# Four places in a four-layer kernel where instructions are put in another order

## Chip, cores and metric

The kernel runs on one core of a Trainium2 chip, as one program. The metric is device time in microseconds (us), lower is better. Instructions are issued in order on each engine: PE (TensorE, the matrix unit), DVE (VectorE), ACT (ScalarE), POOL (GpSimd) and SP (SyncE, which only starts DMA transfers). PE can run at a reduced clock; the profile shows the clock that was granted, 1.00 being full speed.

## The reference

A float32 residual stream `x` of 1024 tokens by 512 features goes through four layers, each added to `x` behind a layer norm without weights:

1. Linear attention with a memory: queries of 8 heads are `elu(q)+1`, multiplied by a memory matrix and divided by a normaliser, then projected.
2. A mixture of 8 low-rank experts (rank 16) beside a dense product. A router takes the two best experts of each token; the dense product has a bias.
3. A Mamba2 layer. An input projection gives gate, x, B, C and dt. x, B and C go through a causal convolution of four taps and silu. In each chunk of 128 tokens y = (C.B times decay) x plus what the chunk before passes on; then y times silu(gate), an RMS norm over 8192 features, and an output projection.
4. A mixture of 4 low-rank experts (rank 8), one per token.

```
def _layernorm(x, axis=-1, eps=1e-05):
    m = jnp.mean(x, axis=axis, keepdims=True)
    v = jnp.var(x, axis=axis, keepdims=True)
    return (x - m) / jnp.sqrt(v + eps)
```

The weight of C.B between tokens s ≤ l of a chunk is exp(cs[l] - cs[s]), with cs the running sum of dt·A. The kernel makes it as exp(-relu(cs[s] - cs[l])); the relu is what is called "clipping" here.

## The kernel before, in words

`x` lies in 8 tiles of 128 tokens by 512 features. Most of the work keeps tokens along the free dimension: `xnT` holds the normalised activations transposed (features on partitions, 1024 tokens free), and PE multiplies against it in 512-token halves.

The code is written for a framework that places the waits: it runs the instructions of an engine in the order in which the program, with a scheduler, puts them, and each waits for the instructions that make its inputs or that still use its buffer. `tc.issue_after(ins)` is a hand-written order: instructions under it are queued behind `ins` on their own engine. Buffers come from pools with a fixed number of copies, so a new tile waits until its buffer's last reader is done.

**First norm (L105 to L125, L308).** For each tile DVE takes statistics (`bn_stats` L108, `bn_aggr` L110), ACT the square root (L112), DVE the reciprocal (L114). The normalised tile `xn` is made on DVE for tiles 0, 3 and 6 (L121) and on ACT for the others (L118 makes its offset on DVE, L119 is the ACT operation). PE transposes four blocks (`ln_ps`, L124) and ACT copies them into `xnT` (L125). L308 calls this tile by tile, and the order on DVE comes out as statistics of several tiles ahead of the rest of the first. Then `zr` is spread (L313) and the queries of 8 heads follow (`ps_q`, L97), whose first half needs `xnT` of tiles 0 to 3. The weights of the output projection are summed on POOL (L295 to L297).

**Attention's projection and second norm (L375 to L397).** PE makes `ps_o` for each tile (L377), DVE adds it to `x` (L392), and the norm of the tile before follows. The norm of tile 7 comes after the loop (L395), then the bias of layer 2 is added to each tile on POOL (L397).

**Router (L148 to L198).** `lora_mixture` runs over the tiles: `f_psl` (L158) gives router scores and low-rank products of a tile, which DVE copies (L165, L166). A callback `ready(t)` can be called ahead of each tile; the first mixture has none. Then `f_pso` (L175), `route_top2` on DVE, transposes (L191) and the expert products (L194).

**Mamba2 (L435 on).** 72 units follow each other: 8 groups, each with one unit for B and C and 8 pairs of heads. `stage_a` of unit n projects (L609), keeps parts of products on ACT (L620), convolves on DVE (L648, L652) and takes silu on ACT (L660, L714, L715). `load_sums` loads 1.5 MB of running sums into `cst` (L726, on SP). `stage_t` of a B/C unit makes C.B on PE (`ps_g`, L740, L747), and from it the tile `gt`: masked on DVE (L757, L763), and copied on ACT (L769). `stage_t` of a pair transposes x (`ps_xt`, L775) and scales it (`xdt` L778, `xdr` L785), then calls `decays` (L797): parts 0 and 1 are 8 clippings each on ACT (L808); part 2 is two exponentials (L814) and two products with `gt` on DVE (L816). `stage_c` multiplies (`ps_y`, L831, L839), adds D·x on DVE (L847) and squares on ACT (L849); `stage_d` multiplies by the gate (L857) and adds the squares to `ssq` (L858). A table `early` (L1005) sets the stages of units 0 to 6; from there on `turn` runs stage_c of n-2 and stage_t of n-1 between the projections of unit n, and `put_off` marks the pairs whose clippings are placed apart.

**Output products and tail.** The output projection of two pairs at a time is seven products `ps_p` (L916), taken in the order 0, 1, 2, 4, 5, 6, 3 and once for each half m. `add_up` (L921) copies each on ACT to a `prod` buffer (L925; three of them) and POOL starts the DMA that adds it to DRAM (L926). In the last unit, `add_up` empties the list `taken` of the last four products behind the last exponential (L1060). After the loop come, in this order, the remaining silu (L1079), the last pair's 16 clippings, `load_prods` (L1086, SP: seven sums loaded as `out10` to `out13`, `out00` to `out03`) and the last two pairs' stages. `put_together` (L944) forms the sums: m=1 on POOL, m=0 on DVE, behind `last["cst"]`. PE meanwhile runs `ps_out` (L1128) of the last four pairs; then come the RMS norm's sums (L1156), `finish` (L1163) of each tile and the last mixture.

```
        with issue_after(last["silu"]):
            for part in range(2):
                decays(N - 1, part)
        with issue_after(last["sums"]):
            load_prods(1)
            load_prods(0)
```

Of the kernel before, what the change touches and what calls it, by code (L numbers as in the profile page):

```python
# [33 lines left out]
P = 128  # L34
# [19 lines left out]
def model_kernel(ctx: ExitStack, tc: tile.TileContext, a: dict, out: bass.AP):  # L54
# [48 lines left out]
                )  # L103

    def layernorm(t, psum, xnp, on_act=False):  # L105

        st = small.tile([P, 6], F32, tag="ln_st", name=f"ln_st{t}")
        nc.vector.bn_stats(st, x[t])  # L108
        mv = small.tile([P, 2], F32, tag="ln_mv", name=f"ln_mv{t}")
        nc.vector.bn_aggr(mv, st)  # L110
        sd = small.tile([P, 1], F32, tag="ln_sd", name=f"ln_sd{t}")
        nc.scalar.activation(sd, mv[:, 1:2], AF.Sqrt, bias=eps, scale=1.0)  # L112
        rs = small.tile([P, 1], F32, tag="ln_rs", name=f"ln_rs{t}")
        nc.vector.reciprocal(rs, sd)  # L114
        xn = xnp.tile([P, DM], F32, tag="xn", name=f"xn{t}")
        if on_act:
            sh = small.tile([P, 1], F32, tag="ln_sh", name=f"ln_sh{t}")
            nc.vector.tensor_scalar(sh, mv[:, 0:1], rs, -1.0, ALU.mult, ALU.mult)  # L118
            nc.scalar.activation(xn, x[t], AF.Identity, bias=sh, scale=rs)  # L119
        else:  # L120
            nc.vector.tensor_scalar(xn, x[t], mv[:, 0:1], rs, ALU.subtract, ALU.mult)  # L121
        ps = psum.tile([P, 512], F32, tag="mm1", name=f"ln_ps{t}")
        for k in range(KT):
            nc.tensor.transpose(ps[:, toks(k)], xn[:, toks(k)], ident)  # L124
        marks["xnT"] = nc.scalar.copy(xnT[:, :, toks(t)], ps.rearrange("p (k t) -> p k t", k=KT))  # L125
# [128 lines left out]
    with ExitStack() as c0:  # L254
# [50 lines left out]
        nc.gpsimd.dma_start(out=f0_up, in_=a["f0_up"])  # L305
        nc.gpsimd.dma_start(out=f0_bias, in_=a["f0_bias"].to_broadcast([P, DM]))

        for t in range(NT):  # L308
            layernorm(t, Both, xns, on_act=t % 3 != 0)


        zr = cw.tile([P, NKV, 32], F32, tag="zr", name="zr")
        nc.vector.tensor_copy(zr, bcast(z, [P, NKV, 32]))  # L313
        sig = [cw.tile([P, NTOK], F32, tag=f"sig{h}", name=f"sig{h}") for h in range(NKV)]

        def queries(h):
# [69 lines left out]
        for t in range(NT):  # L386
# [5 lines left out]
            nc.vector.tensor_tensor(x[t], outs.pop(t), x[t], ALU.add)  # L392
            if t >= 1:
                layernorm(t - 1, Both, act)
        layernorm(NT - 1, Both, act)  # L395
        for t in range(NT):
            nc.gpsimd.tensor_tensor(x[t], x[t], f0_bias, ALU.add)  # L397

        def route_top2(lg):
            E = 8  # L400
# [27 lines left out]
            if t >= 1:  # L428
                layernorm(t - 1, Both, act)

        lora_mixture("f0", 8, 16, f0_base, f0_cat, f0_up, route_top2, Both, act, then_norm)
        layernorm(NT - 1, Both, act)


    with ExitStack() as c1:  # L435
# [9 lines left out]

        last = {"pe": None, "one": None, "two": None, "adt": None, "bar": None, "keep": None, "cst": None, "silu": None, "exp": None, "sums": None}

        def issue_after(ins):  # L450
            return tc.issue_after(ins.ins) if ins else nullcontext()
# [247 lines left out]
        def stage_a(n):  # L699
            kind, i = units[n]  # L700
            raw = b2.tile([P, NTOK], F32, tag="raw", name=f"raw{n}")
            first = xyp.tile([P, NTOK], F32, tag="xy", name=f"xT{n}")
            second = b3.tile([P, NTOK], F32, tag="sg", name=f"sg{n}")
            if kind == "bc":
                raw2 = xyp.tile([P, NTOK], F32, tag="xy", name=f"raw2_{n}")
                pa = yield from project(n, raw, raw2)
                nc.scalar.copy(raw2[:, :512], pa)
                later(n, lambda: conv_silu(raw, 64 + i, first))
                later(n, lambda: conv_silu(raw2, 72 + i, second))
                held[n] = [first, second]  # L710
            else:
                pa = yield from project(n, raw, second)
                later(n, lambda: conv_silu(raw, i, first))
                nc.scalar.activation(second[:, :512], pa, AF.Silu)  # L714
                last["silu"] = nc.scalar.activation(second[:, 512:], second[:, 512:], AF.Silu)  # L715
                held[n] = {"xT": first, "sg": second}
            prefetch(n + 2)
            yield

        def load_sums(n):  # L720

            kind, j = units[n]
            if kind == "bc":
                return
            cst = b2.tile([P, 2, NT + NB, P], F32, tag="cst", name=f"cst{j}")
            last["sums"] = nc.sync.dma_start(  # L726
                out=cst.rearrange("p h c l -> p h (c l)"),
                in_=cs_d[2 * j : 2 * j + 2, :].unsqueeze(0).to_broadcast([P, 2, (NT + NB) * P]),
            )
            held[n].update(cst=cst)  # L730

        def stage_t(n):
            kind, i = units[n]
            if kind == "bc":
                bt, ct = held.pop(n)

                ps = Psum.tile([P, 2, 512], F32, "mm2", f"ps_g0{i}")
                p1 = Psum.tile([P, 512], F32, "mm1", f"ps_g1{i}")
                for b in range(NB):
                    last["pe"] = nc.tensor.matmul(  # L740
                        flat(ps)[:, b * SEQ : (b + 1) * SEQ],
                        lhsT=bt[:, toks(2 * b)],
                        rhs=ct[:, b * SEQ : (b + 1) * SEQ],
                        start=True,
                        stop=True,
                    )
# [16 lines left out]
                nc.vector.tensor_tensor(  # L763
                    gv[:, :, 1, :],
                    p1.rearrange("p (b l) -> p b l", l=P),
                    bcast_mid(tri_le, [P, NB, P]),
                    ALU.mult,
                )
                nc.scalar.copy(gt[:, NT:, :], chunks(flat(ps))[:, :, 1, :])  # L769
                group[i] = gt  # L770
                return
            j, hd = i, held[n]
# [16 lines left out]
                ALU.mult,  # L789
            )  # L790
            hd["xdt"], hd["xdr"] = xdt, xdr
            for part in range(2 if n in put_off else 3):
                decays(n, part)

        decayed, put_off = set(), set()

        def decays(n, part):  # L797


            if not 0 <= n < len(units) or units[n][0] == "bc" or (n, part) in decayed:  # L800
                return
            decayed.add((n, part))
            j, gr = units[n][1], group[units[n][1] // PPG]
            m = held[n]["cst"]
            if part < 2:
                h = 2 * j + part
                for c in range(NT):
                    nc.scalar.activation(  # L808
                        m[:, part, c, :], m[:, part, c, :], AF.Relu, bias=cs[:, c, h : h + 1], scale=1.0
                    )  # L810
                return
            mf = m.rearrange("p h c l -> p h (c l)")
            for hh in range(2):
                last["exp"] = nc.scalar.activation(mf[:, hh], mf[:, hh], AF.Exp, scale=-1.0)  # L814
            for hh in range(2):
                last["cst"] = nc.vector.tensor_tensor(  # L816
                    mf[:, hh], mf[:, hh], gr.rearrange("p c l -> p (c l)"), ALU.mult
                )
# [99 lines left out]

        taken = []

        def add_up():  # L921

            for ps, m, p, over in taken:
                st = osp.tile([P, 512], F32, tag="prod", name=f"prod{over[-1]}_{m}_{p}")
                nc.scalar.copy(st, ps)  # L925
                nc.gpsimd.dma_start(  # L926
                    out=prod_d[m][p // 2][p % 2], in_=st, accum_op=ALU.add if over[0] else ALU.bypass
                )
            taken.clear()

        prods = {}

# [95 lines left out]
        for n in range(len(units)):  # L1028
# [28 lines left out]
            turn(n, 1)  # L1057
            next(a_steps)
            out_products(share - share // 2)
            with issue_after(last["exp"] if n == len(units) - 1 else None):  # L1060
                add_up()
            if share and not todo:
                end_out(began - 1)
            turn(n, 2)
# [3 lines left out]
                    decays(n - 1, 2)  # L1068
            if n == max(early):
                last["bar"] = None  # L1070
            if 1 < n < len(units):
                load_sums(n)


# [2 lines left out]
        N = len(units)  # L1077
        with issue_after(last["silu"]):
            for step in behind_keeps:  # L1079
                last["silu"] = step()  # L1080
        behind_keeps.clear()
        with issue_after(last["silu"]):
            for part in range(2):
                decays(N - 1, part)
        with issue_after(last["sums"]):
            load_prods(1)  # L1086
            load_prods(0)
# [160 lines left out]
```

## Time and profile before

| | us |
|---|---|
| median of 3 runs | 1812.0 (1811.17 to 1812.17) |
| the profiled execution's own time | 1810.48 |
| its span, first to last instruction | 1808.8 |
| PE busy | 1768.5 (98%) |
| DVE busy | 1305.8 (72%) |
| ACT busy | 1187.4 (66%) |
| POOL busy | 721.2 (40%) |

The mean granted clock of PE is 0.996. The span holds 21019 instructions, and the DMA engines move 245.45 MB.

How to read it: times in profile lines are us from the span's start unless marked ns. A timeline line gives start, duration, engine, line of the kernel, operation, output<-inputs, shapes, and how many instructions in a row it sums up (x); in brackets stands how long the engine was idle before and what ended that (`<-DVE xn L121`: it waited for the instruction of line 121 on DVE). The chain of waits is followed back from the last instruction: at each step, to what released it. SPq, DVEq and so on are the engines' sequencers. Matmul ends are modelled, and the rows of one engine overlap slightly for that reason.

### The profile page before, as it was taken

Reading aid. Unit: us, or ns where it says so; the run is one execution under the profiler, and the core shown is the slowest. Engines: PE = TensorE matmul, PEld = TensorE weight load, DVE = VectorE, ACT = ScalarE, POOL = GpSimd, SP = SyncE. Lnnn points to the kernel's source line nnn. Section 1 sums busy time; section 2 is a strip of 40 time slices with the busy share of each in tenths; the row PEclk is TensorE's granted clock in tenths of the full one; section 3 lists DMA queues with packets and bytes.
Section 4 is the critical chain, followed back from the end, with each engine's and each line's share of the span. In section 5 each row is a group of like instructions: output and inputs, shape, how many; then the busy total and the mean of one; then the engine's idle time right before and its main releaser. Section 6 shows DMA issues by size and latency. Waiting matters only on the chain.

```text
span 1808.8 us, 21019 instructions
## 1 busy us (share of the span) xinstructions
PE 1768.5 (98%) x7520; PEld 918.0 (51%) x7520; DVE 1305.8 (72%) x1423; ACT 1187.4 (66%) x2135; POOL 721.2 (40%) x689
## 2 busy tenths in 40 slices
PE   7999988999999999999999999999999999999989
PEld 4445544555555555555555455555555555555554
DVE  4744898886877777777877687868786877777662
ACT  4311369766877588847875777668766877588740
POOL 5410342353444444443444434534444444444220
PEclk9999999999999999999999999999999999999999
DMA  8310134355566545555555446554554566546831
GB/s 314 130 37 24 56 121 152 134 145 117 154 159 150 125 123 147 147 149 145 151 148 146 111 135 157 150 134 135 146 145 112 148 166 149 125 128 152 193 121 47
DMA packets 82810, 245.45 MB, mean 136 GB/s; under 512 B 9921, under 2 KB 10945, under 8 KB 73361
## 3 DMA queue, kind: packets, MB, share of 16 engines
q1 hardware_dynamic: 50240, 175.91, 27.9%
q0 software_dynamic: 31888, 67.14, 21.9%
q8 instruction: 60, 0.98, 0.2%
q10 hardware_dynamic: 576, 1.05, 0.2%
q14 instruction: 46, 0.37, 0.1%
HBM read 182.17 MB, written 61.90 MB: 135 GB/s over the span
## 4 chain that ended last, share of the span: by engine, by line
PE 88%; DVE 5%; ACT 3%; DMA 2%; issue 2%; POOL 1%; SPq 0%; DVEq 0%; ACTq 0%; POOLq 0%
PE pa L609 25%; PE ps_p L916 19%; PE pd L609 12%; PE pb L609 6%; PE ps_y L831 6%; PE ps_o L377 3%; PE ps_q L97 3%; PE ps_xt L775 3%; PE ps_y L839 3%; PE f_pso L175 2%; DVE xT L652 1%; PE f_pso L212 1%; ACT cst L808 1%; PE ps_out L1128 1%; DMA cst<-cs_d 1%
## 5 line engine op out<-in xcount | busy, mean ns | idle before, releaser
L926 POOL DMA_DIRECT2D prod_d<-prod x217 | 189.8, 907 | 583.1 <-ACT prod L925 550.3
L808 ACT ACTIVATE cst<-cst,cs 128x128 f32<-128x128 f32 x1024 | 313.0, 398 | 5.7 <-DMA cst<-cs_d 5.7
L652 DVE SCALAR_TENSOR_TENSOR xT<-raw,convw,xT 128x1020 f32<-128x1020 f32 (+2 forms) x216 | 278.6, 1291 | 4.1
L816 DVE TENSOR_TENSOR cst<-cst,gt 128x1536 f32<-128x1536 f32 x128 | 222.2, 1766 | 13.1 <-ACT cst L814 13.1
L594 POOL TENSOR_TENSOR wsum<-win 128x256 f32<-128x256 f32 x72 | 116.4, 1616 | 264.1 <-DMA win<-in_win 218.6
L849 ACT ACTIVATE xdt<-xT 128x1024 f32<-128x1024 f32 x64 | 67.7, 1058 | 194.1 <-DVE xT L847 194.1
L814 ACT ACTIVATE cst<-cst 128x1536 f32<-128x1536 f32 x128 | 189.4, 1484 | 1.0
L632 DVE TENSOR_TENSOR raw<-pb,keep 128x512 f32<-128x512 f32 x72 | 49.7, 690 | 161.9 <-PE pb L609 158.8
L831 PE MATMUL ps_y<-cst,xdt 128*64 128x128 f32 x2048 | 160.6, 277 | 6.0 <-issue 3.7
L916 PE MATMUL ps_p<-xT,wout 128*128 128x512 f32 x360 | 165.0, 593 | 0.0
L636 DVE TENSOR_TENSOR raw<-pd,keep 128x512 f32<-128x512 f32 x72 | 49.7, 690 | 152.9 <-PE pd L609 125.6
L620 ACT COPY keep<-pa 128x512 f32<-128x512 f32 x144 | 84.8, 589 | 102.6 <-PE pa L609 102.6
L609 PE MATMUL pa<-xnT,wsum 128*128 128x512 f32 x288 | 145.0, 627 | 4.2 <-ACT keep L620 4.2
L831 PEld LDWEIGHTS ps_y<-cst,xdt 128*64 128x64 f32 x2048 | 119.3, 138 | 55.6 <-issue 52.3
L925 ACT COPY prod<-ps_p 128x512 f32<-128x512 f32 x217 | 122.3, 580 | 36.9 <-PE ps_p L916 17.9
L609 PE MATMUL pa<-tok,win 128*128 128x512 f32 x288 | 135.7, 593 | 1.9 <-DVE sg L639 1.9
L609 PE MATMUL pd<-tok,wsum 128*128 128x512 f32 x288 | 136.6, 592 | 0.0
L609 PE MATMUL pa<-xnT,win 128*128 128x512 f32 x288 | 135.8, 592 | 0.6 <-DVE raw L632 0.6
L609 PE MATMUL pa<-tok,wsum 128*128 128x512 f32 x288 | 135.5, 593 | 0.7 <-POOL wsum L597 0.5
L609 PE MATMUL pd<-xnT,wsum 128*128 128x512 f32 x288 | 135.5, 592 | 0.0
L609 PE MATMUL pb<-xnT,win 128*128 128x512 f32 x288 | 135.3, 592 | 0.0
L880 POOL TENSOR_TENSOR osum<-wout,wout 128x256 f32<-128x256 f32 x30 | 106.5, 3553 | 21.4 <-DMA wout<-in_wout 20.9
(228 smaller groups left out, 3111.9 us busy)
## 6 DMA issues: line engine op xcount, KB each, us to landing
cst<-cs_d SPq DMA_DIRECT2D x64, 1536.0 KB, 6.8
prod_d<-prod POOLq DMA_DIRECT2D x217, 256.0 KB, 4.9
win<-in_win SPq DMA_DIRECT2D x144, 256.0 KB, 3.2
wout<-in_wout SPq DMA_DIRECT2D x64, 256.0 KB, 4.1
wo_s<-in_wo POOLq DMA_DIRECT2D x8, 1024.0 KB, 6.0
rb<-rd_d SPq DMA_DIRECT2D x8, 512.0 KB, 4.1
out<-prod_d SPq DMA_DIRECT2D x6, 512.0 KB, 8.7
wq<-in_wq SPq DMA_DIRECT2D x8, 256.0 KB, 4.6
```

The lines of the kernel that those rows point to most:

```text
L594: op(v[:, 0], w[:, 1, 0:2], w[:, 1, 2:4], ALU.add)
L609: last["pe"] = nc.tensor.matmul(ps, lhsT=wt[:, k, :], rhs=tk[:, k, :], start=start and k == 0, stop=k == 1, skip_group_check=not start,)
L620: last["keep"] = nc.scalar.copy(c, ps)
L652: nc.vector.scalar_tensor_tensor(d[:, :, k:], src[:, :, : SEQ - k], convw[:, i, TAPS - 1 - k : TAPS - k], d[:, :, k:], ALU.mult, ALU.add,)
L808: nc.scalar.activation(m[:, part, c, :], m[:, part, c, :], AF.Relu, bias=cs[:, c, h : h + 1], scale=1.0)
L814: last["exp"] = nc.scalar.activation(mf[:, hh], mf[:, hh], AF.Exp, scale=-1.0)
L816: last["cst"] = nc.vector.tensor_tensor(mf[:, hh], mf[:, hh], gr.rearrange("p c l -> p (c l)"), ALU.mult)
L831: last["pe"] = nc.tensor.matmul(flat(py)[e, toks(c)], lhsT=xdt[:, c, e], rhs=m[:, hh, c, :], start=True, stop=c % 2 == 0,)
L880: op(v[:, 0], e[:, 256:], o[:, 256:], ALU.add)
L916: last["pe"] = nc.tensor.matmul(ps, lhsT=w, rhs=y, start=i == over[0], stop=i == over[-1])
L925: nc.scalar.copy(st, ps)
L926: nc.gpsimd.dma_start(out=prod_d[m][p // 2][p % 2], in_=st, accum_op=ALU.add if over[0] else ALU.bypass)
```

## The change

- `layernorm` becomes a generator `norm_steps` in two steps (statistics with square root; the rest). The first norm runs step 1 of tile t, then step 2 of tile t-1, each queued behind the DVE instruction before (`marks["ln"]`); `zr` is queued behind the last. Other callers of `layernorm` run both steps at once.
- The second norm of tile 7 and its bias add move into a callback of the router, called ahead of its tile 3.
- For unit 1, the clippings and what follows are queued behind the copy of `gt` on ACT.
- In the last unit, `load_sums` is called earlier in the program, `add_up` takes three of the four products, then the 16 clippings follow, queued behind the third copy, then the fourth product is copied, queued behind the last clipping. The clippings after the loop are gone.

```
     def layernorm(t, psum, xnp, on_act=False):
+        for _ in norm_steps(t, psum, xnp, on_act):
+            pass
+
+    def norm_steps(t, psum, xnp, on_act=False):
...
-        nc.vector.bn_aggr(mv, st)
+        marks["ln"] = nc.vector.bn_aggr(mv, st)
...
         nc.scalar.activation(sd, mv[:, 1:2], AF.Sqrt, bias=eps, scale=1.0)
+        yield
...
-        for t in range(NT):
-            layernorm(t, Both, xns, on_act=t % 3 != 0)
+        norms = deque()
+        for t in range(NT + 1):
+            if t < NT:
+                norms.append(norm_steps(t, Both, xns, on_act=t % 3 != 0))
+                with tc.issue_after(marks["ln"].ins) if t else nullcontext():
+                    next(norms[-1])
+            if t:
+                with tc.issue_after(marks["ln"].ins):
+                    next(norms.popleft(), None)
...
-        nc.vector.tensor_copy(zr, bcast(z, [P, NKV, 32]))
+        with tc.issue_after(marks["ln"].ins):
+            nc.vector.tensor_copy(zr, bcast(z, [P, NKV, 32]))
...
-        layernorm(NT - 1, Both, act)
-        for t in range(NT):
+        def add_bias(t):
             nc.gpsimd.tensor_tensor(x[t], x[t], f0_bias, ALU.add)
+
+        for t in range(NT - 1):
+            add_bias(t)
+
+        def last_norm(t):
+            if t == 3:
+                layernorm(NT - 1, Both, act)
+                add_bias(NT - 1)
...
-        lora_mixture("f0", 8, 16, f0_base, f0_cat, f0_up, route_top2, Both, act, then_norm)
+        lora_mixture("f0", 8, 16, f0_base, f0_cat, f0_up, route_top2, Both, act, then_norm, last_norm)
...
-                nc.scalar.copy(gt[:, NT:, :], chunks(flat(ps))[:, :, 1, :])
+                last["gt"] = nc.scalar.copy(gt[:, NT:, :], chunks(flat(ps))[:, :, 1, :])
...
-            for part in range(2 if n in put_off else 3):
-                decays(n, part)
+            with issue_after(last["gt"] if n == 1 else None):
+                for part in range(2 if n in put_off else 3):
+                    decays(n, part)
...
-        def add_up():
-
-            for ps, m, p, over in taken:
+        def add_up(most=7):
+
+            for ps, m, p, over in taken[:most]:
...
-                nc.scalar.copy(st, ps)
+                last["prod"] = nc.scalar.copy(st, ps)
...
-            taken.clear()
+            del taken[:most]
...
-            with issue_after(last["exp"] if n == len(units) - 1 else None):
-                add_up()
+            if n == len(units) - 1:
+                load_sums(n)
+                with issue_after(last["exp"]):
+                    add_up(3)
+                with issue_after(last["prod"]):
+                    for part in range(2):
+                        decays(n, part)
+                with issue_after(last["relu"]):
+                    add_up()
+            add_up()
...
-            if 1 < n < len(units):
+            if 1 < n < len(units) - 1:
                 load_sums(n)
...
             for step in behind_keeps:
-                last["silu"] = step()
+                step()
         behind_keeps.clear()
-        with issue_after(last["silu"]):
-            for part in range(2):
-                decays(N - 1, part)
```

`last["relu"]` is the last clipping, and a pair's tiles are now put into `held` piece by piece, since `load_sums` of the last unit comes before its projections are named.

As built, the engines' queues differ from those of the kernel before in this way. DVE: statistics and rest of the first norm alternate; the router's copies of tiles 0 and 1 stand within the norm of tile 7; in the tail the first product with `gt` stands ahead of L857. PE: one `ln_ps` group fewer ahead of the first queries; `f_psl` of tiles 0 to 2 ahead of the last `ln_ps`. ACT: the `gt` copy ahead of unit 1's clippings; the last clippings ahead of the last `prod` copy; one table load less. POOL: three sums of `put_together` ahead of the last store. SP: `out01` is started after `out02`, `out03` and the first `f1_base`.

More of the change, by code (lines that the diff above doesn't have):

```diff
@@ L117, in layernorm @@
             sh = small.tile([P, 1], F32, tag="ln_sh", name=f"ln_sh{t}")
-            nc.vector.tensor_scalar(sh, mv[:, 0:1], rs, -1.0, ALU.mult, ALU.mult)
+            marks["ln"] = nc.vector.tensor_scalar(sh, mv[:, 0:1], rs, -1.0, ALU.mult, ALU.mult)
             nc.scalar.activation(xn, x[t], AF.Identity, bias=sh, scale=rs)
         else:
-            nc.vector.tensor_scalar(xn, x[t], mv[:, 0:1], rs, ALU.subtract, ALU.mult)
+            marks["ln"] = nc.vector.tensor_scalar(xn, x[t], mv[:, 0:1], rs, ALU.subtract, ALU.mult)
         ps = psum.tile([P, 512], F32, tag="mm1", name=f"ln_ps{t}")
@@ L444, in tile @@
                 return {"mm2": psum2, "mm1": psum1, "in": psumi}[tag].tile(shape, dt, tag=tag, name=name)
-        last = {"pe": None, "one": None, "two": None, "adt": None, "bar": None, "keep": None, "cst": None, "silu": None, "exp": None, "sums": None}
+        last = {"pe": None, "one": None, "two": None, "adt": None, "bar": None, "keep": None, "cst": None, "silu": None, "exp": None, "sums": None, "gt": None, "prod": None, "relu": None}
         def issue_after(ins):
@@ L715, in stage_a @@
                 last["silu"] = nc.scalar.activation(second[:, 512:], second[:, 512:], AF.Silu)
-                held[n] = {"xT": first, "sg": second}
+                held.setdefault(n, {}).update(xT=first, sg=second)
             prefetch(n + 2)
@@ L729, in load_sums @@
             )
-            held[n].update(cst=cst)
+            held.setdefault(n, {})["cst"] = cst
         def stage_t(n):
@@ L807, in decays @@
                 for c in range(NT):
-                    nc.scalar.activation(
+                    last["relu"] = nc.scalar.activation(
                         m[:, part, c, :], m[:, part, c, :], AF.Relu, bias=cs[:, c, h : h + 1], scale=1.0
```

## Prediction

> **What bounds the kernel now.** The page first. It gives TensorE (PE) 1768.5 us busy in a span of 1808.8, and its chain of waits says which engine the end was waiting for:
>
> ```profile
> PE 88%; DVE 5%; ACT 3%; DMA 2%; issue 2%; POOL 1%; SPq 0%; DVEq 0%; ACTq 0%; POOLq 0%
> ```
>
> PE issues the same matmuls in both kernels (only their order moves), so an edit is worth what it takes off PE's gaps and late start (1808.8 - 1768.5 = 40 us in all) and off its half-speed stretches. I therefore read the timeline of PE, then those of ACT, DVE and POOL, at the four places of the change. From 14 to 140 us and from about 330 to 1710 us PE hardly stops, so time won ahead of such a stretch stays won.
>
> The chain of waits, the first norm:
>
> ```profile
> 11.90 0.56 ACT xnT L125
> 12.46 0.71 ACT xn L119
> 13.18 0.97 ACT xnT L125 x2
> 14.19 2.84 PE ps_q L97 x6
> ```
>
> The first query waits for the copies of tiles 2 and 3, and ACT makes an xn between them. Timeline of PE, the router:
>
> ```profile
> 139.48 0.60 PE L124 MATMUL ln_ps<-ident,xn 128*128 128x128 f32 x4
> 142.55 0.66 PE L124 MATMUL ln_ps<-ident,xn 128*128 128x128 f32 x4 [2.47 <-DVE xn L121]
> 143.04 7.58 PE L158 MATMUL f_psl<-f_cat,xnT 128*128 128x136 f32 x64
> ```
>
> PE stands 2.47 us for the last norm with the router of seven ready tiles behind it. Timeline of ACT, then of PE, at the first C.B:
>
> ```profile
> 253.99 0.69 ACT L808 ACTIVATE cst<-cst,cs 128x128 f32<-128x128 f32 x2 [3.15 <-DMA cst<-cs_d]
> 254.59 1.04 ACT L660 ACTIVATE xT<-xT 128x1024 f32<-128x1024 f32 x1
> 255.53 0.39 ACT L808 ACTIVATE cst<-cst,cs 128x128 f32<-128x128 f32 x1
> 255.83 0.56 ACT L769 COPY gt<-ps_g 128x512 f32<-128x512 f32 x1
> ```
>
> ```profile
> 256.44 1.97 PE L775 MATMUL ps_xt<-ident,xT 128*128 128x128 f32 x8 [4.18 <-ACT gt L769]
> ...
> 278.40 3.68 PE L609 MATMUL pa<-xnT,wsum 128*128 128x512 f32 x4 [2.77 <-ACT keep L620]
> ```
>
> ACT waits 3.15 us for a load, and the gt copy that PE needs is queued behind that wait. The tail, timelines of ACT, POOL, DVE and PE:
>
> ```profile
> 1715.08 0.58 ACT L925 COPY prod<-ps_p 128x512 f32<-128x512 f32 x1 [4.43 <-DMA prod_d<-prod]
> ...
> 1716.99 4.77 ACT L808 ACTIVATE cst<-cst,cs 128x128 f32<-128x128 f32 x16
> ```
>
> ```profile
> 1721.89 1.28 POOL L950 TENSOR_TENSOR out<-out,out 128x512 f32<-128x512 f32 x1 [0.18 <-DMA out<-prod_d]
> 1723.24 2.15 POOL L951 TENSOR_TENSOR out<-out,out 128x512 f32<-128x512 f32 x1
> ```
>
> ```profile
> 1722.74 1.50 DVE L857 SCALAR_TENSOR_TENSOR xT<-xT,normw,sg 128x1024 f32<-128x1024 f32 x1 [5.86 <-ACT xdt L849]
> 1724.17 2.30 DVE L858 TENSOR_TENSOR ssq<-ssq,xdt 128x1024 f32<-128x1024 f32 x1
> ...
> 1728.12 5.05 DVE L816 TENSOR_TENSOR cst<-cst,gt 128x1536 f32<-128x1536 f32 x2
> ```
>
> ```profile
> 1733.23 0.90 PE L831 MATMUL ps_y<-cst,xdt 128*64 128x128 f32 x5 [2.29 <-DVE cst L816]
> ```
>
> ACT waits 4.43 us for a store, the 16 clippings stand behind it, and PE ends up waiting for DVE's two products of them.
>
> **Part 1, first norm: 0.4 us gained (-1.3 to +1.0).** No instruction is added. DVE now finishes tile t-1 before the statistics of t+1. I walked the three queues with the rows' durations (statistics 0.66, aggregate 0.17, 1/sd 0.14, sd 0.29, xn 0.53 on DVE and 0.81 on ACT, copy 0.56, 0.04 between dependents) and the landings of x (4.6 to 8.9). The first transpose comes near 6.9 instead of 8.82. But ACT's queue still ends sd5, xn4, xnT2, xnT3: from 11.2 on, 0.2 + 0.8 + 0.5 + 0.6 is 13.2, against 14.15 measured (14.06 in the same walk of the old order). One transpose group fewer stands before the first query, one more inside the queries; by the time the fourth 512-token half starts, the walk has 18.05 against 18.42: 0.4. Upper end, the 1.0 of the first query. Lower end: the transposes now come in pieces from 6.9 on, and the clock may still be halved at 13.2. The shortest half-speed stretch in the clock's record is 3.41 us (278.48 to 281.90); one of that length loses half of it, 1.7, less the 0.4 gained: -1.3. The zr copy moved behind the norm is read by L336, tens of us later; POOL's L296 sums end near 62, before L368 needs them at 73.
>
> **Part 2, last norm within the router: 2.3 (1.9 to 2.5).** The same instructions; the 64 router passes take 7.42 (143.04 to 150.46), 0.93 a tile. Tiles 0 to 2 now run 139.92 to 142.70. The chain of tile 7 is add 0.70, statistics 0.70, aggregate 0.20, sd 0.30, 1/sd 0.17, xn 0.56; two pairs of DVE copies (0.45 in all) now lie in it, so xn7 is ready at about 142.97, the transposes start at 143.0 (0.49 to the next row, as before), and five tiles (4.64) end at 148.13 instead of 150.46. What is late next is the DVE chain of the route: it ends at 157.32, 3.4 before L191 at 160.76, and both shift together, so L175 still covers it. The bias add of tile 7 keeps its place as POOL's last. If the clock dropped in the gap it would show in the row at 143.04, and it did not.
>
> **Part 3, C.B copy ahead: 1.7 (0.8 to 3.3).** On ACT the order becomes silu, silu, gt, 16 clippings. L757 ends at 253.91; gt runs 253.95 to 254.51, ps_xt starts at 254.55 (1.89 earlier). Queued behind gt are the clippings: their load lands at 253.99, so they lose 0.4 of start, but the second silu now sits in the wait; their two exps end at 263.4 instead of 264.4. Next late is ACT itself: keep L620, which ended the 2.77 gap, comes at 277.1, 1.3 earlier. ps_y ends 1.9 earlier or, if the half-speed stretch that followed the gap goes too, up to 3.3. Between ACT's 1.3 and PE's 1.9 lies 1.7 with the earlier load of the next cst; the lower end is ACT's 0.95 with nothing else, rounded down. Windows of PE's clock (columns: stretch, PE, PEld, DVE, ACT, POOL busy, clock, DMA share, GB/s):
>
> ```profile
> 276.00:278.00 2.00, 0.00 (x0) 0.00 (x0) 2.00 (x2) 2.00 (x3) 0.00 (x0) 1.00 0.76 240
> 279.00:280.00 1.00, 1.00 (x2) 0.34 (x1) 1.00 (x1) 0.30 (x1) 0.00 (x0) 0.50 0.90 381
> ```
>
> After a gap of 2.77 us PE ran at 0.50; after 2.47 (at 142.55) it did not. [...]
>
> **Part 4, clippings ahead of the last copy: 0.3 (-1.5 to +4.6).** ACT: the load of cst63 lands at 1712.45, so the clippings run 1712.5 to 1717.2, 4.5 earlier. The copy of product 3 follows at 1717.15 (2.1 later); the second ps_out bank is freed by it at 1717.7, 0.5 after PE wants it, and xT's silu is done at 1719.2. Both waits are covered, since DVE takes ps_xt only at 1726. The exps end at 1722.0 and 1724.3 (3.5 and 2.6 earlier), one table load saved. DVE: the first product with gt now stands ahead of L857 and waits for the first exp, with L857, L858, xdt and xdr queued behind. Its work from 1722 to the second product is 2 x 1.76 (the mean of L816 on the page) + 1.28 + 1.22 + 1.21 + 0.68 = 7.9 alone: end 1729.9. But here L816 took 2.32 and 2.83 and L858 2.30, while POOL's L951 took 2.15 and its L954 2.78 against 1.27 for its L949; the ends of one engine's operations meet the other's starts. DVE and POOL take turns, so with POOL's 10.4 us of work in the same place DVE ends at 1731 to 1733.8 against 1733.17 now. I take 1732.9, near the late end, since the second L816 (2.83) lay beside L954 (2.78) and POOL's queue isn't earlier: 0.3. The lower end is 0.6 (1733.8) and 0.9 for the store's issue, now between POOL's sums; the upper is 3.3 (1733.2 less 1729.9) and half of ps_y's half-speed stretch (1733.23 to 1735.97), 1.3.
>
> [...]
>
> The store of product 3 goes past three POOL sums: it leaves at about 1723.2 instead of 1715.95, and lands after 6.8 (this one's time before) at 1730; SP's out01 load behind it (4.06) lands at 1734, now issued behind out03 and f1_base1. DVE's L951 needs it at 1735.2. It is hidden, by 1 us.
>
> **Sum.** 0.4 + 2.3 + 1.7 + 0.3 = 4.7. The profiled execution took 1810.48 (span 1808.8): 1805.8. The median of 1812.0 lies 1.5 above it, so 1807.3. A measurement of this kernel can tell about 0.2%, 3.6 us, from no change.
>
> **Rivals.**
> - The tail carries: DVE's products slip in ahead of POOL's sums, the second ends at 1729.9, PE's gap shrinks below 2.47 and ps_y keeps its clock. 4.6 in place of 0.3: 9.0 in all, 1803.0. For: POOL's sums start only as loads land (1720.4, 1721.9). Against: the rows of alternation. 0.15.
> - The gains shrink: the queries start at half clock (-1.3) and ACT holds part 3 at 0.8 to 1.0. 2.3 + 0.9 + 0.3 - 1.3 = 2.2, about 1809.8, within 0.2%. For: ACT's idle stretch after the clippings is small. Against: in the trace the transposes fell from 0.213 to 0.107 us at about 12.2, 3.4 after the first; now the first is 6.3 ahead of the query. 0.21.
> - Slower: the late store. With 10.1 us to land (as the store of product 6 took, 1709.00 to 1719.10) it lands at 1733.3; an out01 load of 12.5 (as out10, 1703.99 to 1716.48) ends at 1745.8, 10.6 behind L951. The last pair's L847, L857 and L858 are queued behind it on DVE, and PE's L1156 waits for those: the other parts' 4.4 less 10.6 is 6 lost, about 1818. It decides from L951 past 1743.2 (1735.2 + 4.4 + 3.6). Against: three stores were in flight then, and here there is one. 0.07.
> - That the change doesn't do what it says is ruled out: the built order of each engine has all four moves and no other.
>
> **How the numbers follow.** My forecast, 1807.3, has 0.57 (its own range 1804.5 to 1808.8); the cases above have 0.15, 0.21 and 0.07. The range 1803.0 to 1810.4 leaves out the slower case and the outer parts of the two beside it. Faster by over 0.2% is the forecast, all but 0.04, and the first rival: 0.68; within 0.2% is the second and that 0.04: 0.25; slower 0.07.
>
> **What would show it.** Part 1: first query at 13.0 to 13.3 and at full clock. Part 2: no gap above 0.5 ahead of ln_ps7, f_pso starting 2.3 earlier relative to L377's end. Part 3: ps_g to ps_xt under 2.5 us; ps_y of pair 0 ending 1.9 to 3.3 earlier, and less of it left by 330. Part 4: second L816 ending about as long after ps_y62 as now; if 3 earlier, the first rival. It is wrong if the stretch from 330 to 1710, with the same instructions, changes its length, or if a late out01 row stands before L951.

## The result, and the profile after

The changed kernel took 1808.03 us (median of 12 runs, 1806.44 to 1809.41) against 1812.07 of before in the same session (12 runs, 1809.82 to 1814.28): a ratio of 0.9978, 95% interval 0.9969 to 0.9987, or 4.0 us. The forecast was 4.7. The two profiled executions lie closer to each other: 1810.48 before (1.6 under its median) and 1809.27 after (1.2 over), spans 1808.8 and 1807.6. So the sum came out nearly as forecast, but the traces have to say whether its terms did, and why one execution tells so little.

Times at five places, from the timelines of PE, give the account of the two profiled executions:

| stretch | before | after | gained |
|---|---|---|---|
| start to ln_ps6 of the second norm | 139.48 | 141.25 | -1.77 |
| ln_ps6 to the first f_pso | 10.98 | 8.56 | 2.42 |
| first f_pso to the last ps_p | 1557.89 | 1556.19 | 1.70 |
| last ps_p to two_banks | 34.22 | 33.62 | 0.60 |
| two_banks to the end | 66.21 | 67.95 | -1.74 |

The lines behind it, of the kernel after. The timeline of PE at the start:

```profile
7.05 1.09 PE L129 MATMUL ln_ps<-ident,xn 128*128 128x128 f32 x4 [7.05 <-DVE xn L126]
8.92 3.08 PE L129 MATMUL ln_ps<-ident,xn 128*128 128x128 f32 x12 [0.79 <-ACT xn L124]
12.59 1.12 PE L129 MATMUL ln_ps<-ident,xn 128*128 128x128 f32 x4 [0.59 <-ACT xn L124]
13.55 3.78 PE L97 MATMUL ps_q<-xnT,wq 128*128 128x512 f32 x4
```

The first transposes come 1.77 earlier and the first query 0.64 earlier, but its four matmuls take 3.78; before, six took 2.84. By these durations, 0.95 each against 0.47, they run at half speed. The trace's record of the clock begins with the rise to full speed: 12.24 before, 17.84 here. Timeline of PE, the router:

```profile
141.69 2.95 PE L163 MATMUL f_psl<-f_cat,xnT 128*128 128x136 f32 x24
144.71 0.63 PE L129 MATMUL ln_ps<-ident,xn 128*128 128x128 f32 x4
145.17 4.80 PE L163 MATMUL f_psl<-f_cat,xnT 128*128 128x136 f32 x40
149.81 10.46 PE L180 MATMUL f_pso<-f_base,xnT 128*128 128x512 f32 x24
```

The wait of 2.47 us is gone; ln_ps7 stands between the passes of tiles 2 and 3. Timeline of PE at the first C.B:

```profile
253.90 1.09 PE L796 MATMUL ps_xt<-ident,xT 128*128 128x128 f32 x8 [2.32 <-ACT gt L790]
...
276.38 2.96 PE L630 MATMUL pa<-xnT,wsum 128*128 128x512 f32 x4 [4.20 <-ACT keep L641]
```

The wait for gt fell from 4.18 to 2.32 and no half speed followed it (8 transposes in 1.09 against 1.97). The later wait grew from 2.77 to 4.20: PE came sooner, ACT's keep did not by as much. Timelines of DVE, POOL and PE in the tail:

```profile
1720.21 1.76 DVE L838 TENSOR_TENSOR cst<-cst,gt 128x1536 f32<-128x1536 f32 x1 [5.69 <-ACT cst L836]
1721.89 2.29 DVE L879 SCALAR_TENSOR_TENSOR xT<-xT,normw,sg 128x1024 f32<-128x1024 f32 x1
1724.10 2.28 DVE L880 TENSOR_TENSOR ssq<-ssq,xdt 128x1024 f32<-128x1024 f32 x1
...
1728.04 2.31 DVE L838 TENSOR_TENSOR cst<-cst,gt 128x1536 f32<-128x1536 f32 x1
```

```profile
1720.23 2.87 POOL L972 TENSOR_TENSOR out<-out,out 128x512 f32<-128x512 f32 x1
1723.04 0.88 POOL L948 DMA_DIRECT2D prod_d<-prod  x1
1723.65 1.65 POOL L973 TENSOR_TENSOR out<-out,out 128x512 f32<-128x512 f32 x1
```

```profile
1716.00 5.42 PE L1155 MATMUL ps_out<-wout,xT 128*128 128x512 f32 x12 [0.88 <-ACT prod L947]
...
1739.62 1.92 PE L1183 MATMUL two_banks<-ones,ssq 128*128 128x1 f32 x16 [1.04 <-DVE ssq L880]
1741.40 1.91 PE L1155 MATMUL ps_out<-wout,xT 128*128 128x512 f32 x2
```

DVE's L879, L880 and second L838 next to POOL's sums still take 2.29, 2.28 and 2.31 in place of the 1.28, 1.22 and 1.76 that the prediction counted for DVE alone. And two_banks has a wait of 1.04 that was not there before, after which two matmuls take 1.91 in place of 1.10: half speed again, with a granted clock of 0.50. The timeline of PE before, at the same place:

```profile
1742.57 1.84 PE L1156 MATMUL two_banks<-ones,ssq 128*128 128x1 f32 x16
1744.27 1.10 PE L1128 MATMUL ps_out<-wout,xT 128*128 128x512 f32 x2
```

Windows of the kernel after (stretch, PE, PEld, DVE, ACT, POOL busy, clock, DMA share, GB/s) show it in the third column from the end:

```profile
1738.00:1741.00 3.00, 1.96 (x15) 1.41 (x13) 1.48 (x2) 0.32 (x1) 0.00 (x0) 1.00 0.01 3
1742.00:1744.00 2.00, 2.00 (x7) 1.24 (x6) 0.08 (x1) 0.00 (x0) 0.00 (x0) 0.50 0.02 4
```

### The profile page after: what moved, and what is told of

It is laid out like the page before. It is cut to its first block, busy times and chain, and to the rows that moved or that the text cites. A ratio compares the mean times of both kernels' runs of the same rounds, so it can differ in the third digit from the quotient of the medians.

```text
span 1807.6 us, 21018 instructions
## 1 busy us (share of the span) xinstructions
PE 1771.8 (98%) x7520; PEld 918.1 (51%) x7520; DVE 1305.9 (72%) x1423; ACT 1188.0 (66%) x2135; POOL 720.6 (40%) x689
## 4 chain that ended last, share of the span: by engine, by line
PE 87%; DVE 6%; ACT 3%; issue 2%; DMA 2%; POOL 1%; SPq 0%; DVEq 0%; POOLq 0%; ACTq 0%
PE pa L630 25%; PE ps_p L938 19%; PE pd L630 12%; PE pb L630 6%; PE ps_y L853 5%; PE ps_q L97 3%; PE ps_o L391 3%; PE ps_xt L796 3%; PE ps_y L861 2%; DVE xT L673 2%; PE f_pso L180 2%; PE f_pso L217 1%; ACT cst L830 1%; DMA prod_d<-prod 1%; PE ps_out L1155 1%
## 5 line engine op out<-in xcount | busy, mean ns | idle before, releaser
L838 DVE TENSOR_TENSOR cst<-cst,gt 128x1536 f32<-128x1536 f32 x128 | 221.2, 1758 | 19.8 <-ACT cst L836 19.8
```

The source lines that it names most:

```text
L838: last["cst"] = nc.vector.tensor_tensor(mf[:, hh], mf[:, hh], gr.rearrange("p c l -> p (c l)"), ALU.mult)
```

## The experiments

Theory 1: part 1 loses by the clock, since PE's transposes now come in pieces; parts 2 and 3 gain as worked out; in part 4 POOL's sums take from DVE what ACT gave. Its rivals stand in the expectations. Ratios are against the kernel before in the same session, with 95% intervals; a ratio of 0.001 is 1.8 us. `ln_ps6` is the start of the transposes of tile 6 in the second norm, and the last column runs from the start of the last `ps_p` to the end of the span; both are from the one profiled execution of each run.

| run | median us | ratio | ln_ps6 | last ps_p to end |
|---|---|---|---|---|
| part 1 alone | 1813.65 | 1.0004 (0.9995 to 1.0012) | 141.63 | 102.25 |
| part 2 alone | 1809.18 | 0.9980 (0.9971 to 0.9989) | 139.40 | 102.44 |
| part 3 alone | 1810.45 | 0.9989 (0.9980 to 0.9997) | 139.44 | 102.37 |
| part 4 alone | 1811.42 | 0.9992 (0.9984 to 1.0001) | 139.38 | 100.39 |
| parts 2 to 4 | 1807.83 | 0.9977 (0.9967 to 0.9987) | 139.60 | 99.70 |
| all, idle transposes | 1812.39 | 1.0003 (0.9995 to 1.0012) | 144.13 | 100.72 |
| all, ACT's order held | 1806.83 | 0.9973 (0.9963 to 0.9984) | 139.17 | 99.92 |
| all, ps_out ahead | 1806.17 | 0.9965 (0.9952 to 0.9977) | 141.43 | 97.96 |
| all, no sums on POOL | 1803.22 | 0.9952 (0.9938 to 0.9966) | 140.84 | 95.22 |
| all, sums on DVE | 1803.48 | 0.9950 (0.9936 to 0.9963) | 141.19 | 95.65 |
| that, idle transposes | 1801.47 | 0.9942 (0.9930 to 0.9955) | 139.20 | 95.26 |
| sums on DVE, old norm | 1802.30 | 0.9949 (0.9936 to 0.9963) | 139.41 | 95.91 |

**Each part alone.** The kernel before with the lines of one part of the diff.

> Only the first norm's new order. Theory 1 (the clock): the transposes now come in pieces, so the clock rises later than the first query; in the changed kernel's trace full speed came at 17.84 us, and ln_ps6 of the second norm started 1.77 later than before. Here too: full speed after 14, second norm's ln_ps6 0.5 to 2 later than before's 139.48, time 0 to 2 us above before. Rival (queue order): the gain of 0.4 that the walk of the queues gave is there in most executions and the profiled one was unlucky: time 0.4 below before, ln_ps6 at about 139.1.

Full speed came at 18.45 and ln_ps6 2.15 later. The time rose by 0.7 us, with 0 inside the interval. Theory 1 by the trace; the timed loss is smaller and not clear of noise. This run also showed something on part 2, since it keeps the wait that part 2 takes away. Timeline of PE, and windows around it:

```profile
144.70 1.11 PE L129 MATMUL ln_ps<-ident,xn 128*128 128x128 f32 x4 [2.47 <-DVE xn L126]
145.60 6.63 PE L163 MATMUL f_psl<-f_cat,xnT 128*128 128x136 f32 x45
```

```profile
141.00:144.00 3.00, 1.23 (x6) 0.50 (x4) 1.67 (x4) 0.88 (x2) 0.00 (x0) 1.00 0.00 0
145.00:147.00 2.00, 2.00 (x11) 2.00 (x10) 0.00 (x0) 1.14 (x2) 1.00 (x1) 0.50 0.00 0
```

It is the same wait of 2.47 us as before, and here the clock fell to 0.50 behind it (144.74 to 148.16 in the record).

> Only the norm of tile 7 within the router. Theory 1: the wait of 2.47 us goes to under 0.2, f_pso starts 2.3 to 2.5 earlier against the last ps_o, and this stays to the end: time 2.4 below before. Rival: the earlier start is given back at the DVE-bound stretch of the time steps or at the load of the first running sums, so the time falls by less than 1.

ln_ps6 to f_pso 8.56 (10.98): 2.42, and the time fell by 3.6 (2.0 to 5.3). Theory 1; its 2.4 lies inside the interval. If the gain is more, the half speed that follows the wait in some executions fits: ln_ps6 to f_pso took 12.64 with it in the run of part 1 alone, and 10.98 in the three other profiles that keep the wait.

> Only the gt copy ahead of unit 1's clippings. Theory 1: gap ahead of ps_xt 4.18 to 2.3, no half speed there, ACT's keep then ends a gap that is longer than 2.77 (4.2), and 1.7 remain at 300 us: time 1.7 below before. Rival: the longer second gap costs as much clock as the first saved, and less than 0.7 remains.

Wait ahead of ps_xt 2.32, no half speed there; the time fell by 2.0 (0.5 to 3.6). Theory 1, but the rival's 0.7 is just inside the interval, and the wait of the old order is not the same in every execution. Timelines of PE in the run of part 1 alone, then of part 2 alone, both with the old order here:

```profile
259.27 1.09 PE L789 MATMUL ps_xt<-ident,xT 128*128 128x128 f32 x8 [3.22 <-ACT gt L783]
```

```profile
253.53 1.09 PE L782 MATMUL ps_xt<-ident,xT 128*128 128x128 f32 x8 [3.79 <-ACT gt L776]
```

No half speed followed these two, and the later wait for the keep was 4.22 in both, as long as with the new order. Half speed followed the 4.18 of before and the 3.53 of part 4 alone. From the first f_pso to the last ps_p the four profiles with the old order took 1557.0 to 1557.9, the ten with the new one 1556.2 to 1556.8. So the new order is worth 0.2 to 1.7 by the traces, the most where the clock had fallen.

> Only the last clippings ahead of the last copy. Theory 1: DVE's second product with gt ends about 0.5 earlier against the last ps_y of pair 62, since DVE and POOL take turns; two_banks starts 0.5 to 0.8 earlier, and in some executions a half-speed stretch of 3.4 follows it, which costs 1.7: time 0.8 below to 1 above before. Rival (ACT's 3.5 us come through): second product 3 us earlier, time 3 below.

The second product ends no earlier (17.58 after L847 of pair 62 began, 17.57 before), with L857 and L858 at 2.28 each; last ps_p to end 100.39. The time fell by 1.4 (-0.2 to 2.9). So DVE is held up beside POOL's sums as theory 1 has it (1.28 and 1.22 in the run without them, below), and the rival's 3 us are not there; theory 1's 0.5 is not there against before either. The gain is 0.6 more than it allowed, inside an interval that holds 0. The three runs above, with the old tail, took 102.25 to 102.44 on this way, with 6.83 us of half speed in it, and their second products ended 18.0 to 18.3 after L847 of pair 62 began; the profiled execution of before took 100.43, with 3.41 of half speed, and this run had none ahead of the last matmuls. So the tail of before was a lucky one against those three, and part of what part 4 seems to save is the clock.

**Part 1 left out.**

> The changed kernel with the first norm in its old order (the other three parts stay). Theory 1 (pieces of transposes keep the clock low): full speed at 12 to 15 us, the second norm's ln_ps6 back at 139.4 (141.25 in the changed kernel), time 1.8 to 2.2 below the changed kernel, about 6 below before. Rival (the changed kernel's profiled start was one bad execution): within 0.5 of the changed kernel.

Full speed at 11.84, ln_ps6 at 139.60, the profiled span 3.3 shorter. But the ratio of the timed runs is that of the changed kernel to 0.0001. In the trace it is theory 1; in the timed runs the loss isn't seen.

**Idle transposes on PE.** The edit, at the head of the first norm (the first run had 28 ahead and 2, 2, 1 behind):

```
+        idle = Both.tile([P, 2, 512], F32, "mm2", "idle")
...
+                        marks["tr"] = nc.tensor.transpose(flat(idle)[:, :P], ident, ident)
```

> The changed kernel with idle transposes of the identity on PE, into a bank that nothing reads: 28 from the start of the program, 2, 2 and 1 behind the first three tiles. Theory 1: the clock is full before the first query (before 9 us), the query starts at 13.0 to 13.3 and runs at full speed, ln_ps6 comes at 138.8 to 139.2, time 2.2 to 2.5 below the changed kernel. Rival (the order of the queues, not the clock, made the start late): ln_ps6 stays at 141, time as the changed kernel.

A miss, by my edit: the scheduler put all eight square roots ahead of ACT's first copy, four more than in the changed kernel. That copy came at 13.70, PE waited 3.90 us, and the clock, full at 7.18, fell again from 14.01 to 20.84. It tells the two theories apart only in that a full clock before the query did not last through this wait of 3.90. The second try ties the square roots of tiles 4 and 5 behind the copies of tiles 0 and 1:

> The changed kernel with idle transposes of the identity on PE (26 ahead of the first tile; 4, 4 and 2 behind the first three), and two square roots tied behind copies so that ACT's and PE's order of the real work stays that of the changed kernel. Theory 1 (the clock makes the start late): full speed before 9 us and no half-speed stretch until the first query, which comes at 13.0 to 13.4 and takes 0.86 a pass; ln_ps6 of the second norm at 138.8 to 139.3 (141.25 in the changed kernel, 139.4 in the old order); time 2 below the changed kernel. Rival (the order of the queues makes it late): ln_ps6 at 140.8 to 141.6 again.

Timeline of PE of this run:

```profile
12.62 0.66 PE L131 MATMUL ln_ps<-ident,xn 128*128 128x128 f32 x4 [1.24 <-ACT xn L126]
13.57 1.98 PE L98 MATMUL ps_q<-xnT,wq 128*128 128x512 f32 x4 [0.30 <-ACT xnT L134]
```

The query starts at the same time as in the changed kernel (13.57, 13.55), with the same order, and takes 1.98 instead of 3.78. ln_ps6 comes at 139.17. So in the traces it is the clock, and not the queues, that loses part 1's gain; with the clock up the new order is worth 0.2 to 0.4 against the old one (139.38 to 139.60 in six profiles). The timed runs say less: by the ratios this kernel is 0.9 below the changed one, where 2 was expected, and the intervals overlap.

**The tail.** First, ps_out of the last pair ahead of two_banks:

```
+        with issue_after(last["pe"]):
+            for t in range(3):
+                out_project(t, NPAIR - 1)
```

> The changed kernel with the last pair's ps_out of tiles 0 to 2 (2.6 us of PE) put ahead of two_banks, which waits for ssq. Theory 1 (a wait of 1.0 and eight one-column products make an idle window): the wait of 1.04 ahead of two_banks is gone, and so is the half-speed stretch after it; the way from the last ps_p to the end shortens from 101.6 to 98.8 to 100, the median by 1 to 2.5 against the changed kernel. Rival (rms, needed by the first finish, now comes later and holds DVE): no gain.

Timeline of PE:

```profile
1736.72 4.54 PE L1155 MATMUL ps_out<-wout,xT 128*128 128x512 f32 x10
1741.09 1.84 PE L1186 MATMUL two_banks<-ones,ssq 128*128 128x1 f32 x16
```

The wait and the half speed behind two_banks are gone; last ps_p to end 97.96, less than the 98.8 to 100 expected. The ratio is 0.0013 lower, 2.4 us, with overlapping intervals. Theory 1 by the trace, though not every execution has that wait: two profiles without this edit (parts 2 to 4, and ACT's order held) had neither it nor the half speed behind two_banks. Their way took 99.7 and 99.9, still 1.7 or more above this. Next, the changed kernel without `put_together(1)`, whose result lacks these sums:

> The changed kernel without the seven sums on POOL (put_together of m=1 is left out, so its rows of the output projection are wrong by those sums). Theory 1 (DVE and POOL take turns): L879 1.28, L880 1.22, second L838 1.76 in place of 2.29, 2.28 and 2.31, and it ends 2.5 earlier, at about 17.5 us after the last ps_y of pair 62 began its wait; PE's wait ahead of ps_y63 shrinks, and part 4's gain grows by 1.5 to 2.5. Rival (the slow rows come from DMA or from their operands): the same durations as in the changed kernel.

Timeline of DVE:

```profile
1719.26 1.76 DVE L838 TENSOR_TENSOR cst<-cst,gt 128x1536 f32<-128x1536 f32 x1 [4.74 <-ACT cst L836]
1720.94 1.28 DVE L879 SCALAR_TENSOR_TENSOR xT<-xT,normw,sg 128x1024 f32<-128x1024 f32 x1
1722.14 1.22 DVE L880 TENSOR_TENSOR ssq<-ssq,xdt 128x1024 f32<-128x1024 f32 x1
...
1725.01 1.75 DVE L838 TENSOR_TENSOR cst<-cst,gt 128x1536 f32<-128x1536 f32 x1
```

Every operation has its short duration, and the second product ends at 1726.76 instead of 1730.35, the last ps_p being at 1706.00 in both. From the first product's start to the second's end DVE took 7.5, against 10.14 in the changed kernel; the four profiles with no sums on POOL took 7.5, the six that have this order and the sums 10.1 to 10.9. So POOL's sums cost DVE 2.6 us here, near the 2.5 expected. Theory 1. The other 0.95 of the 3.6 is an earlier start of the first product, and that start varies by itself (13.1 to 14.5 after the last ps_p in those six). Then the sums on DVE, behind the last ssq, with six ps_out to cover them:

```
-            op = (nc.gpsimd if m else nc.vector).tensor_tensor
+            op = nc.vector.tensor_tensor
...
-        parts = {1: put_together(1)}
+        parts = {}
...
+        with issue_after(last["ssq"]):
+            parts[1] = put_together(1)
```

> The changed kernel with the seven sums of m=1 taken from POOL and put on DVE behind the last ssq, and six of the last pair's ps_out ahead of two_banks, which cover them. Theory 1 (POOL's sums stood in DVE's way): L879, L880 and L838 at 1.28, 1.22 and 1.76 as without the sums; last ps_y 23.4 after the last ps_p (27.0 in the changed kernel), end 94 to 95 after it (101.6); time 5 to 7 below the changed kernel. Rival (the sums only change places: 4.3 us on DVE delay the finish by as much): end 98 or later after the last ps_p, time as with the ps_out ahead alone.

Same short rows; last ps_y 24.1 after the last ps_p, end 95.65 after it, 1803.48. The last ps_y is 0.7 later than theory 1 gave, the end 0.65 past its range, the time 5.1 below the changed kernel by the ratios, at its weak end; the mechanism is as it said: all the sums are done, and the way is 5.9 shorter than the changed kernel's. Of these 5.9 the run with three ps_out ahead already had 3.6, so 2.3 are left for the sums and the three more ps_out.

> Both of the other two edits together. If both theories hold, 2 below the kernel with the sums on DVE, about 1800 to 1801; if the start's edit does nothing, the same as that kernel.

1801.47, the fastest of all: 10.5 below before by the ratio. Against the kernel with the sums on DVE that is 1.5 by the ratios, where 2 was expected, with overlapping intervals; in the trace ln_ps6 comes 2.0 earlier (139.20, 141.19).

> The kernel with the sums on DVE and six ps_out ahead of two_banks, with the first norm back in its old order and no idle transposes. Theory 1 (the first norm's new order is worth 0.3 to 0.4 only where the clock is kept up, and costs about 1.9 where it isn't): full speed at 12 to 15 us, ln_ps6 at 139.4 to 139.6, time 1801.5 to 1802.2, within 0.7 of the kernel with all edits and about 1.7 below the one with the sums alone. Rival (the new order costs nothing in the timed runs): the same as the kernel with the sums alone, 1803.5.

1802.30, between the two theories, and by the ratio (0.9949) the same as with the new norm (0.9950). The trace is as theory 1 has it, with full speed at 11.96 and ln_ps6 at 139.41; the timed runs do not settle it.

## Why the prediction was right, and where it was not

**The sum was right, 4.0 measured for 4.7, but not term by term, and so in part by luck.**

- **Part 1 (0.4 gained, -1.3 to +1.0): the term that failed, at -1.77 in the profiled execution.** It gave the four query passes full speed and bounded the other case by one half-speed stretch of 3.41, less the gain. In the five profiles that have the new order without idle work, full speed came at 17.11 to 18.45 and ln_ps6 at 140.84 to 141.63: 1.2 to 2.3 later than the old order's 139.38 to 139.60. The half-speed stretch of the kernel after reaches from before the query to 4.3 us into it (13.55 to 17.84). The queue walk itself was good (first query 13.55, walked 13.2). What the timed runs lose by it is not settled: 0.7 in the run of part 1 alone and 0.2 by the two pairs of ratios with and without it, each within its interval. One number on record could hide a loss: the mean granted clock of the timed runs, which counts from the clock's first record on and so leaves out the slow start (the window from 14 to 17 us of the kernel after has 1.00, where the queries' matmuls took 0.95 each). It is higher with the new norm in all three comparisons: 0.9955 against 0.9949 (part 1 alone, before), 0.9975 against 0.9963 (changed kernel, part 1 left out), 0.9988 against 0.9984 (sums on DVE, with the old norm). That is 0.7 to 2.1 us less lost at half speed, and a loss of 0.9 to 2.3 outside it. This is an estimate from those means, which counts all half speed as lost work; where that half speed fell, and why there was less of it, no run shows.
- **Part 2 (2.3): right at 2.42 in the trace.** The sentence that a drop of the clock "would show in the row at 143.04, and it did not" took one execution for all. The same wait was followed by 0.50 in the run of part 1 alone; alone, part 2 gave 3.6 (2.0 to 5.3), from which 2.3 can't be told.
- **Part 3 (1.7): right in size, 1.70 in the trace and 2.0 alone, with luck in the trace.** The pair shows the most that this stretch gains: before's clock had fallen behind the wait for gt (0.50 from 254.59 to 261.41), and against the two profiles where it had not the new order gains 0.2 to 1.1. The wait ahead of ps_xt came out as worked out (2.3), the keep 1.4 earlier beside the shift of 0.65 (1.3 worked out). The half speed behind the second wait stayed, as that wait grew; it was as long in the two runs of the old order whose clock had not fallen.
- **Part 4 (0.3): right that POOL's sums hold DVE up, the size not pinned down.** L879, L880 and L838 again took 2.29, 2.28 and 2.31 beside these sums, and 1.28, 1.22 and 1.75 in the run without them. The second product ends 17.10 after L869 of pair 62 began, 17.57 (L847) before: 0.5 earlier. But one pair says little: six profiles of this order have 16.3 to 18.2, part 4 alone among them with 17.58, and four of the old one 17.6 to 18.3. The first rival's 1803.0 needed POOL's sums out of the way, and the run without them shows that price: 2.6 of DVE's time. The late store was hidden: out01 landed at 1730.59, and DVE wanted it at 1733.45. The wait for the ps_out bank was 0.88 (0.5 worked out) and covered. Not foreseen was the wait ahead of two_banks, 1.04 in three of the five profiles that keep this tail, with half speed behind two of them.
- **The profiled execution as the base.** The sum was made against 1810.48, whose tail had half the half-speed time of the three other profiles with that tail. The tail of the changed kernel (99.7 to 101.6 in five profiles that keep it) is worth 0.7 to 2.7 against their 102.3 to 102.4. That, and part 2, may have made good in the median what part 1 lost. Alone, the parts gave -0.7, 3.6, 2.0 and 1.4, together 6.3 for the 4.0 measured, which their intervals allow. The changed kernel's 12 runs had a mean granted clock of 0.9975, before's runs of the later sessions 0.9949 to 0.9959: by the estimate above up to 2.9 to 4.7 us less lost at half speed, as much as the whole gain, where the sum counted mostly waits. How the 4.0 divides between waits and clock is not shown.

**Idle time of PE and the clock.** The prediction set the 2.77 us after which PE ran at 0.50 against the 2.47 after which it did not. The length of the wait did not decide in these runs: one of 2.47 was followed by 0.50 in the run of part 1 alone, and one of 3.79 in the run of part 2 alone was not.

## What to carry to other kernels

Work taken forward on one engine is worth only what the next engine on the way can take: find out which it is, and whether a neighbour (here POOL's sums, which cost DVE 2.6 us) stands in its way, before you count the gain. Spreading a cold start's work out in time can lose more by the clock than the earlier start gains: here the first query came 0.64 us earlier, and ln_ps6 1.77 later. Cover the holes with idle work, with which ln_ps6 came at 139.17 in place of 141.25, and check that the scheduler leaves the real order alone. Where PE has waits of 2 to 4 us, as here, read several executions: the same wait of 2.47 was followed by half speed in one profile and not in another.

## What the runs showed of the hardware

**The clock of PE.** The traces of the kernels before and after record a granted clock of 1.00 or 0.50. These are the half-speed stretches behind the first record, without the one that begins 1.15 us ahead of the end in both, with the time that PE was busy in the 3.41 us ahead of each:

| kernel | at 0.50 | us | PE busy in the 3.41 us ahead (share) |
|---|---|---|---|
| before | 254.59 to 261.41 | 6.83 | 1.09 (0.32) |
| before | 278.48 to 281.89 | 3.41 | 0.64 (0.19) |
| before | 1732.56 to 1735.97 | 3.41 | 0.40 (0.12) |
| after | 277.25 to 280.66 | 3.41 | 0.86 (0.25) |
| after | 1724.50 to 1727.91 | 3.41 | 1.47 (0.43) |
| after | 1741.57 to 1744.98 | 3.41 | 2.37 (0.70) |

All these changes lie whole multiples of 3.4133 us from the first record of their trace (12.24 before, 17.84 after), to within 0.01: at 71, 73, 78, 79, 504 and 505 of them before, at 76, 77, 500, 501, 505 and 506 after. What sets this spacing is not shown. Cut into the same steps, the least busy one at full speed behind the first record that no half speed followed is that from 138.53 before (1.55 us busy, 0.45), then those from 249.95 after (0.48) and 285.31 before (0.50). The step of 0.70 holds the 16 one-column products of two_banks, 1.92 us of its 2.37; whether they count for less than others, no run tests. In the one half-speed stretch of 6.83, PE was busy for 1.56 of the first 3.41 and for all of the second.

**What a wait cost.** The wait of 2.47 us lay before in a step with 1.55 us busy, and the clock stayed at 1.00; in the run of part 1 alone PE was busy for 1.23 of the 3.00 us from 141 on, and the clock was 0.50 from 144.74 to 148.16. The wait of 4.18 for gt was followed by 6.83 us at 0.50 before. By an estimate that takes half of each such stretch as lost, waits of 2 to 4 us thus cost nothing, 1.7 or 3.4 us of clock. The wait for the keep, 2.77 before and 4.20 after, was followed by 3.41 at 0.50 in both.
